# A fourth layer rebuilt in five stage lanes, with elementwise work moved off GpSimd

## The chip, the cores and the metric

The kernel runs on one NeuronCore of a Trainium2 chip. It is one launch: the residual goes in with channels first and comes out in the same form. The metric is the device time of that launch in microseconds, the median of several runs. The engines are called PE (TensorE matmul), PEld (its weight loads), DVE (VectorE), ACT (ScalarE), POOL (GpSimd) and SP (SyncE), as in the profile. All data are fp32.

## The reference

Four layers, each a macaron: half a feed-forward, a mixing block, half a feed-forward, with the residual `x` (4 batches of 1024 tokens, 128 channels) running through. Layers 0 to 2 are a mixture of experts with attention over heads, a gated feed-forward with attention over tokens, and a mixture of experts with decayed linear attention. The change is in layer 3:

```python
x = x + 0.5 * _L3_ffn_ref(_layernorm(x), ...)
x = x + _L3_attn_ref(_layernorm(x), ...)
x = x + 0.5 * _L3_ffn_ref(_layernorm(x), ...)

# _L3_ffn_ref: x_prev is x one token earlier
xr = mu_r * x + (1.0 - mu_r) * x_prev
xk = mu_k * x + (1.0 - mu_k) * x_prev
out = sigmoid(xr @ W_r.T) * (square(relu(xk @ W_k.T)) @ W_v.T)

# _L3_attn_ref: 16 heads of 8 channels
xx = xs - x                                   # xs is x one token earlier
m = tanh((x + xx * time_maa_x) @ time_maa_w1)       # five groups of 32
mw, mk, mv, mr, mg = einsum("btfe,fec->fbtc", m, time_maa_w2)
xw = x + xx * (time_maa_w + mw)               # xk, xv, xr, xg likewise
r, k, v = xr @ W_r, xk @ W_k, xv @ W_v
g = silu(xg @ W_g)
w = time_decay + tanh(xw @ time_decay_w1) @ time_decay_w2
# per token, S is 8x8 for each head, wd = exp(-exp(w)):
#   y = r . (S + u * k v);   S = S * wd + k v
yn = groupnorm(y) * ln_gamma + ln_beta
out = yn * g @ W_o
```

## The kernel before, in words

The residual lies in four SBUF tiles `X[b]` of 128 channels by 1024 tokens. Layer 3 works on halves of 512 tokens (`HALF`); I call one batch and one half a unit, so there are eight units, and half 1 of a batch follows half 0.

`normed` (L919) is a layer norm in this form: a product with the centering matrix, `Square` and a copy on ACT, four products of 128 tokens with a column of means (`n_sq`), `Sqrt` on ACT and a reciprocal on DVE, four products that spread the result over channels (`n_r`), and a DVE product that gives `xn`. Column 0 of `xn` is the last token of the half before (or zero), set by POOL, so that `xn[:, 0:512]` is "one token earlier".

`l3_ffn` (L959) does both halves of a batch: a norm, four products that mix the present and the past token in the weights, three ACT functions, one more product, a DVE product, and the addition to the residual on POOL (L984).

`l3_time` (L999) does a half in this order. `xx` on POOL (L1012), `xxx` on DVE, the low-rank products, and four products of 32 rows, `w2`, into four PSUM banks of the pool `wave`. `mixed` (L1027) forms each of the five inputs on DVE and then adds `x` on POOL (L1030). The projections give `wdec`, `k`, `vals`, `r`, `g`. Then the recurrence: the 8 x 8 state of the 16 heads is laid out as 8 columns `j` of 128 partitions each. For each of two waves, four products of 32 rows (`vrows`) spread a column of `vals` into four banks; for each of the four, DVE multiplies it with `k` (`kv`, L1066), a scan along the tokens gives the state `st` (L1072), POOL copies a column in (L1071) or out (L1076), and POOL multiplies `st` with `r` into `z` (L1078). Four products of 32 columns (`sums`) then add the `z` of a wave into quarters of one accumulator `acc`. The finish is a group norm on `y`, a product with `g` on POOL (L1101), two products with `W_o`, and the addition to the residual on DVE.

The order of the work is set in two steps. Each function is a generator that yields costs; `lanes` (L1111) always runs on the lane whose summed cost is lowest, and so fixes the order in which the program is written down. A planner then puts every engine's instructions into one fixed queue, earlier written ones first where it expects them to be ready; it lets layer 3's first instructions in between those of layer 2's last experts. On the chip each engine works its queue in order. In layer 3 there are two lanes (L1239 to L1246): batches 0 and 2 with their tiles on the left of SBUF, batches 1 and 3 on the right, each with two PSUM banks, and four banks (`wave`) shared. The mixture of experts of layer 2 has its tiles on the left and the four PSUM banks `main`; layer 2's attention and layer 1's feed-forward had their tiles on the right and the four banks `side`.

The last three parts of layer 2 are `experts` for batches 2 and 3 (39 blocks, each with a 578 KB weight load, L455, an indirect gather, L457, and an indirect scatter, L442) and `combine` (L476). Batches 0 and 1 have their final residual before these experts begin.

Of the kernel before, what the change touches and what calls it, by code (L numbers as in the profile page):

```python
# [12 lines left out]
AF = mybir.ActivationFunctionType  # L13
ALU = mybir.AluOpType
AX = mybir.AxisListType

P = 128
# [4 lines left out]
HALF = 512  # L22
# [183 lines left out]
class Macaron:  # L206
# [712 lines left out]
    def normed(self, ps, wp, b, h, before):  # L919
# [5 lines left out]
        sq, xc = self.t(wp, [P, HALF], "n_sq", bufs=1), self.t(wp, [P, HALF], "n_xc", bufs=1)  # L925
# [5 lines left out]
        std, r = self.t(wp, [P, 4], "n_std"), self.t(wp, [P, 4], "n_r")  # L931
# [5 lines left out]
        xn = self.t(wp, [P, HALF + 1], "xn")  # L937
        if before is None:
            nc.gpsimd.memset(xn[:, 0:1], 0.0)
        else:  # L940
            nc.gpsimd.tensor_copy(xn[:, 0:1], before[:, HALF:])
# [17 lines left out]
    def l3_ffn(self, ps, wp, m, b):  # L959
        nc = self.nc  # L960
        bank = lambda: self.t(ps, [P, HALF], "bank")
        xn = None
        for h in range(2):
            X = self.X[b][:, h * HALF : (h + 1) * HALF]
            xn = self.normed(ps, wp, b, h, xn)
            yield 3
            x, xp = xn[:, 1:], xn[:, 0:HALF]

            def mixed(k):
                o = bank()  # L970
                self.mm(o, m["now" + k], x, stop=False)
                self.mm(o, m["past" + k], xp, start=False)
                return o

            r, k, y = (self.t(wp, [P, HALF], tag, bufs=1) for tag in ("r", "k", "y"))
            k2 = self.t(wp, [P, HALF], "kv")
            nc.scalar.activation(k, mixed("k"), AF.Relu)
            nc.scalar.activation(k2, k, AF.Square)
            nc.scalar.activation(r, mixed("r"), AF.Sigmoid)
            yield 4  # L980
            o = bank()
            self.mm(o, m["wv"], k2)
            nc.vector.tensor_tensor(y, r, o, ALU.mult)
            nc.gpsimd.tensor_tensor(X, X, y, ALU.add)  # L984
            yield 2
# [13 lines left out]
    def l3_time(self, ps, wave, wp, m, c3, b):  # L999
        nc = self.nc  # L1000
        v, act, pool = nc.vector, nc.scalar.activation, nc.gpsimd
        bank = lambda shape=(P, HALF): self.t(ps, list(shape), "bank")
        four = lambda: [self.t(wave, [P, HALF], "wave") for _ in range(4)]
        one = lambda tag, rows=P, bufs=1: self.t(wp, [rows, HALF], tag, bufs=bufs)
        xn = carry = None
        for h in range(2):
            X = self.X[b][:, h * HALF : (h + 1) * HALF]
            xn = self.normed(ps, wp, b, h, xn)
            yield 3
            x, xp = xn[:, 1:], xn[:, 0:HALF]  # L1010
            xx, xxx = one("xx"), one("xxx")
            pool.tensor_tensor(xx, xp, x, ALU.subtract)  # L1012
            v.scalar_tensor_tensor(xxx, xx, m["maa"][:, 0:1], x, ALU.mult, ALU.add)
            lo, hi = one("lo"), one("hi", 32)
            lp = bank()
            self.mm(lp, m["w1"][:, 0:P], xxx)
            act(lo, lp, AF.Tanh)
            hp = bank((32, HALF))
            self.mm(hp, m["w1"][:, P : P + 32], xxx)
            act(hi, hp, AF.Tanh)  # L1020
            yield 4
            mp = four()
            for f in range(4):
                rows = slice(32 * f, 32 * f + 32)
                self.mm(mp[f], m["w2"][rows, :], lo[rows, :])

            def mixed(f, mp):  # L1027
                t = one("mix", bufs=3)
                v.scalar_tensor_tensor(t, mp, m["maa"][:, f + 1 : f + 2], xx, ALU.add, ALU.mult)
                pool.tensor_tensor(t, t, x, ALU.add)  # L1030
                return t
# [253 lines left out]
```

## Time and profile before

| | |
|---|---|
| median of 3 runs | 3297.95 us (3294.87 to 3299.5) |
| profiled execution | 3388.92 us |
| its span | 3387.1 us |
| granted TensorE clock over the span | 0.888 |
| PE, PEld, DVE | 2861.4, 1672.3, 1793.1 us busy |
| ACT, POOL | 1614.4, 973.6 us busy |

The profiled execution is about 2.8% longer than the runs without a profile. A row of groups gives the engine, the operation, what it writes and reads, the shape, the count, the busy time, the mean time of one, and the idle time of the engine ahead of them with what ended it. `x128` of a PE group counts two passes for each fp32 product. The profile tells two PE groups apart only by their tiles, since most products are written in one helper line (L227). Where busy times of several PE records overlap, the busy time is that of their union.

### The profile page before, as it was taken

The numbers are of one execution on the slowest core, as the hardware profiler recorded it, in microseconds if no ns is written. First come the engines' busy times: TensorE is split into PE (matmuls) and PEld (weight loads), VectorE is DVE, ScalarE is ACT, GpSimd is POOL, SyncE is SP. The second block draws the span as 40 slices with busy tenths as digits, with TensorE's granted clock in tenths as the row PEclk, the third lists the DMA queues.
The fourth block names the chain that finished last, engine by engine and source line by source line (L and its number), as shares of the span: only waits on it lengthen the run. The fifth ranks groups of instructions, "written<-read, shape, count | busy, mean of one in ns | idle before, by whom it ended". The sixth has DMA issues, their size and how long they took to land.

```text
span 3387.1 us, 48419 instructions
## 1 busy us (share of the span) xinstructions
PE 2861.4 (84%) x18126; PEld 1672.3 (49%) x18126; DVE 1793.1 (53%) x3048; ACT 1614.4 (48%) x3546; POOL 973.6 (29%) x972
## 2 busy tenths in 40 slices
PE   6777758778779999999999998987968877688887
PEld 6655547556533333333333335676757856223323
DVE  3387776853136776776776742434454422354353
ACT  4555525567404665665665663454423444322432
POOL 2465506433330000000000000353404444254353
PEclk7888959889879999999999998998978979687888
DMA  5565516544400000000000000475624656000000
GB/s 169 166 186 172 174 45 188 168 123 134 149 13 2 6 6 4 6 6 16 6 6 3 1 1 18 135 218 170 185 71 144 193 166 188 13 0 7 7 0 13
DMA packets 122890, 277.64 MB, mean 82 GB/s; under 512 B 18016, under 2 KB 67296, under 8 KB 122528
## 3 DMA queue, kind: packets, MB, share of 16 engines
q1 hardware_dynamic: 101792, 231.77, 23.1%
q0 software_dynamic: 20864, 42.77, 4.1%
q8 instruction: 144, 2.36, 0.3%
q14 instruction: 90, 0.74, 0.1%
HBM read 238.43 MB, written 31.85 MB: 80 GB/s over the span
## 4 chain that ended last, share of the span: by engine, by line
PE 68%; DVE 13%; POOL 5%; issue 5%; ACT 5%; DMA 4%; another core or an unknown queue 0%; SPq 0%; POOLq 0%; DVEq 0%; ACTq 0%
PE bank L227 37%; PE two L227 16%; PE o L227 8%; PE s L227 4%; DMA c_y<-res 2%; DVE nm L717 2%; POOL z L1078 1%; DMA res<-e_y,g_target 1%; DVE prod L542 1%; ACT e_h L468 1%; DVE sc L527 1%; POOL res L442 1%; DVE prod L525 1%; PE bank L461 1%; PE wave L227 1%
## 5 line engine op out<-in xcount | busy, mean ns | idle before, releaser
L717 DVE TENSOR_REDUCE nm<-two 128x2 f32<-128x1024 f32 x512 | 626.8, 1224 | 289.2 <-PE s L227 269.8
L740 ACT ACTIVATE e<-s 128x512 f32<-128x512 f32 x1024 | 555.8, 595 | 403.5 <-PE s L227 400.5
L468 ACT ACTIVATE e_h<-bank,e_w 128x128 f32<-128x128 f32 x1304 | 453.3, 367 | 544.2 <-PE bank L227 445.6
L227 PE MATMUL bank<-e_x,e_w 128*128 128x128 f32 x2608 | 573.0, 318 | 152.4 <-ACT e_h L468 61.5
L227 PE MATMUL s<-qm,kz 32*128 32x512 f32 x2048 | 633.5, 642 | 0.8 <-ACT e L740 0.8
L227 PE MATMUL two<-kz,qz 32*128 32x512 f32 x2048 | 592.1, 663 | 19.5 <-DVE nm L717 2.5
L457 POOL DMA_INDIRECT e_xg<-rows,g_source x326 | 328.5, 1008 | 942.1 <-DVE g_target L412 347.5
L227 PEld LDWEIGHTS bank<-e_x,e_w 128*128 128x128 f32 x2608 | 413.8, 203 | 290.4 <-ACT e_h L468 124.3
L442 POOL DMA_INDIRECT res<-e_y,g_target x326 | 376.1, 1154 | 319.5 <-DVE e_y L441 179.9
L227 PE MATMUL bank<-e_w,e_h 128*128 128x128 f32 x2608 | 450.7, 289 | 15.7 <-ACT e_h L468 12.9
L227 PEld LDWEIGHTS bank<-e_w,e_h 128*128 128x128 f32 x2608 | 378.4, 202 | 29.5 <-ACT e_h L468 22.3
L227 PE MATMUL o<-e,va 128*32 128x256 f32 x4096 | 328.3, 392 | 0.1
L441 DVE TENSOR_TENSOR e_y<-bank,e_w 128x128 f32<-128x128 f32 x326 | 94.4, 290 | 438.3 <-PE bank L227 379.5
L227 PEld LDWEIGHTS two<-kz,qz 32*128 32x128 f32 x2048 | 159.3, 188 | 237.5 <-issue 161.0
L227 PEld LDWEIGHTS o<-e,va 128*32 128x32 f32 x4096 | 81.0, 108 | 389.6 <-issue 370.3
L227 PEld LDWEIGHTS s<-qm,kz 32*128 32x128 f32 x2048 | 206.5, 183 | 11.4 <-issue 7.7
L705 POOL COPY va<-vd 128x256 f32<-128x256 f32 x16 | 6.7, 432 | 624.4 <-PE o L227 538.1
L463 DVE COPY e_x<-bank 128x128 f32<-128x128 f32 x326 | 92.8, 285 | 93.6 <-PE bank L461 73.2
L493 PE MATMUL bank<-c,c_y 128*128 128x128 f32 x128 | 39.5, 453 | 111.8 <-DVE c_y L490 111.8
L227 PE MATMUL bank<-g_cols,g_lanes 128*128 128x39 f32 (+1 forms) x512 | 83.3, 321 | 25.5 <-DVE g_cols L392 24.8
L1078 POOL TENSOR_TENSOR z<-st,r 128x512 f32<-128x512 f32 x64 | 96.0, 1503 | 22.7 <-DVE st L1072 22.4
L461 PE MATMUL bank<-c,e_xg 128*128 128x128 f32 x326 | 94.5, 290 | 7.6 <-DMA e_xg<-rows,g_source 7.6
(302 smaller groups left out, 3778.1 us busy)
## 6 DMA issues: line engine op xcount, KB each, us to landing
e_w<-in_l0m_dram SPq DMA_DIRECT2D x170, 578.0 KB
e_w<-in_l2m_dram SPq DMA_DIRECT2D x156, 578.0 KB
c_y<-res SPq DMA_DIRECT2D x32, 512.0 KB
rows<-g_xt SPq DMA_DIRECT2D x16, 512.0 KB
e_xg<-rows,g_source POOLq DMA_INDIRECT x326
res<-e_y,g_target POOLq DMA_INDIRECT x326
x<-in_x_dram SPq DMA_DIRECT2D x4, 512.0 KB
qz<-qd SPq DMA_DIRECT2D x64, 32.0 KB
```

Source lines behind the costliest of these rows:

```text
L227: self.nc.tensor.matmul(out, lhsT, rhs, start=start, stop=stop)
L441: nc.vector.tensor_tensor(y, o, w[:, MOE_W - D :], ALU.add)
L442: ins = nc.gpsimd.indirect_dma_start(out=res[:, :], out_offset=at(target[:, k : k + 1]), in_=y, in_offset=None)
L457: nc.gpsimd.indirect_dma_start(out=xg, out_offset=None, in_=rows[:, :], in_offset=at(source[:, k : k + 1]))
L461: nc.tensor.transpose(tp, xg, self.c0["ident"])
L463: nc.vector.tensor_copy(x, tp)
L468: nc.scalar.activation(h[:, fc, :], up[:, fc, :], func, bias=w[:, 2 * FC * P + fc : 2 * FC * P + fc + 1])
L493: nc.tensor.transpose(tp[:, j, :], y[1][:, i, :], self.c0["ident"])
L525: v.tensor_tensor(pr, q.unsqueeze(2).to_broadcast(sh), k.unsqueeze(1).to_broadcast(sh), ALU.mult)
L717: v.tensor_reduce(nm[:, it, h, 2 * pair : 2 * pair + 2], s, AX.X, ALU.max, negate=True)
L740: nc.scalar.activation(es[g], s, AF.Exp, scale=scale)
L1078: pool.tensor_tensor(z, st[:, 0:HALF], r, ALU.mult)
```

## The change

`l3_time` is cut into three functions, and layer 3 gets five lanes in place of two: one that runs the recurrences of all units, two for the ends of even and odd batches (`l3_finish` and the second feed-forward) and two for their fronts (the first feed-forward and `l3_prepare`). A lane's part is one unit, not one batch. A recurrence waits for its `prepare`, a finish for its recurrence.

Pools: the fronts' tiles lie on the right of SBUF and the recurrence's and the ends' on the left; PSUM has 2 banks for the broadcasts, 1 for `acc`, 2 shared by the ends, 3 shared by the fronts. `g` and `y` have two buffers, the other results of `l3_prepare` one for each of the two fronts.

Moved from POOL: `xx`, the residual addition of the feed-forward, the product with `g`, every second `z` and the memsets go to DVE; the column copies go to ACT. The addition of `x` in `mixed` is left out, and the weight is applied twice in one accumulation, once to `x` and once to the rest. The `w2` products come in pairs in place of fours, as do the broadcasts. A helper, `together`, ties a list of products to one another in PE's queue (and optionally behind another product); the sums of a wave come in fours, behind the next pair of broadcasts.

```diff
-    def normed(self, ps, wp, b, h, before):
+    def normed(self, ps, tmp, wp, b, h, before):
...
-        xn = self.t(wp, [P, HALF + 1], "xn")
+        xn = self.t(wp, [P, HALF + 1], "xn", bufs=3)
         if before is None:
-            nc.gpsimd.memset(xn[:, 0:1], 0.0)
+            nc.vector.memset(xn[:, 0:1], 0.0)
         else:
-            nc.gpsimd.tensor_copy(xn[:, 0:1], before[:, HALF:])
+            nc.scalar.copy(xn[:, 0:1], before[:, HALF:])
...
-            nc.vector.tensor_tensor(y, r, o, ALU.mult)
-            nc.gpsimd.tensor_tensor(X, X, y, ALU.add)
+        nc.vector.tensor_tensor(r, r, o, ALU.mult)
+        nc.vector.tensor_tensor(X, X, r, ALU.add)
...
+    def together(self, matmuls, after=None):
+
+        order = mybir.DependencyInfo(mybir.DependencyClass.NoSync, mybir.DependencyReason.DATA)
+        for out, lhsT, rhs, start, stop in reversed(matmuls):
+            i = self.nc.tensor.matmul(out, lhsT, rhs, start=start, stop=stop).ins
+            if after is not None:
+                self.tc.add_manual_dep(i, after.name, order, reason="side by side")
+            after = i
+        return after
...
+    def l3_prepare(self, ps, tmp, wp, m, c3, b, h, seen, out):
...
+        v.tensor_tensor(xx, xp, x, ALU.subtract)
...
+            if fs == (4,):
+                self.mm(mp[0], m["w2l"], hi)
+            else:
+                self.together([(mp[i], m["w2"][rows[i], :], lo[rows[i], :], True, True) for i in range(2)])
...
+        def project(w, share=None, rows=P, alone=None):
+            o = bank((rows, HALF))
+            if share is None:
+                self.mm(o, w, alone)
+            else:
+                self.mm(o, w, x, stop=False)
+                self.mm(o, w, share, start=False)
+            return o
...
+    def l3_recur(self, wave, ps, wp, c3, b, h, carries, given):
...
+        for w in range(2):
+            zs = []
+            for pair in range(2):
+                js = [4 * w + 2 * pair + i for i in range(2)]
+                vb = [self.t(wave, [P, HALF], "wave") for _ in js]
+                rows = [slice(32 * (j % 4), 32 * (j % 4) + 32) for j in js]
+                last = self.together([(vb[i], c3["vrows"][rows[i], w, :], vals[rows[i], :], True, True) for i in range(2)])
+                for sums in held:
+                    self.together(sums, last)
+                held = []
+                kv = []
+                for i in range(2):
+                    kv.append(self.t(wp, [P, HALF], "kv", bufs=3))
+                    v.tensor_tensor(kv[i], k, vb[i], ALU.mult)
+                for i, j in enumerate(js):
                     st = self.t(wp, [P, HALF + 1], "st", bufs=3)
-                    if last is None:
-                        pool.memset(st[:, 0:1], 0.0)
+                    if h == 0:
+                        v.memset(st[:, 0:1], 0.0)
                     else:
-                        pool.tensor_copy(st[:, 0:1], last[:, j : j + 1])
+                        nc.scalar.copy(st[:, 0:1], carry[:, j : j + 1])
                     v.tensor_tensor_scan(
...
                     if h == 0:
-                        pool.tensor_copy(carry[:, j : j + 1], st[:, HALF:])
-                    z = one("z", bufs=6)
-                    pool.tensor_tensor(z, st[:, 0:HALF], r, ALU.mult)
+                        nc.scalar.copy(carry[:, j : j + 1], st[:, HALF:])
+
+                    z = self.t(wp, [P, HALF], "z", bufs=6)
+                    (pool if i else v).tensor_tensor(z, st[:, 0:HALF], r, ALU.mult)
                     zs.append(z)
...
+            held.append([(acc[32 * q : 32 * q + 32, :], c3["sums"][:, w, :], zs[q], w == 0, w == 1) for q in range(4)])
+        for sums in held:
+            self.together(sums)
+        v.tensor_tensor(y, y, acc, ALU.add)
...
+    def l3_finish(self, ps, wp, m, c3, b, h, given):
...
-            pool.tensor_tensor(yc, yc, g, ALU.mult)
+        v.tensor_tensor(yc, yc, g, ALU.mult)
...
+    def layer3(self, f, t, c3):
...
+            wave, accs, tail, prep = (
+                enter(self.psum(name, n)) for name, n in (("l3wave", 2), ("l3acc", 1), ("l3tail", 2), ("l3prep", 3))
+            )
+
+            tmp, *front = (enter(sb(name, side="right")) for name in ("l3tmp", "l3even", "l3odd"))
+            rec, *end = (enter(sb(name)) for name in ("l3rec", "l3ends0", "l3ends1"))
...
+            units = [(b + i, h) for b in range(0, B, 2) for h in range(2) for i in range(2)]
+            fronts, recs, ends = ([], []), [], ([], [])
+            for b, h in units:
...
+            self.lanes(recs, *ends, *fronts)
```

## The prediction

> **What bounds the kernel now.** I read the page's forty slices first, then the table of stretches over the last 650 us, then the groups of the last layer, and last the timeline inside one recurrence. Times below are us from the span's start. The slices say where the kernel is weak:
>
> ```profile
> span 3387.1 us, 48419 instructions
> ...
> PE   6777758778779999999999998987968877688887
> ...
> PEclk7888959889879999999999998998978979687888
> ```
>
> A slice is 84.7 us, so the last six, from 2880 on, are the last layer. PE is at 6 to 8 tenths at a granted clock of 6 to 8 tenths there: it is neither full nor fast. I cut that part into stretches at the turns of the recurrence (the span in which `st` and `z` are made); columns are the length, then busy us and instructions of PE, PEld, DVE, ACT, POOL, then PEclk, DMA share, GB/s:
>
> ```profile
> 2735.00:2868.00 133.00, 114.64 (x738) 95.86 (x737) 25.59 (x87) 68.48 (x179) 72.58 (x77) 0.93 0.62 191
> ...
> 2888.00:2952.00 64.00, 49.27 (x116) 21.13 (x116) 12.34 (x21) 22.69 (x33) 13.69 (x16) 0.69 0.00 0
> 2952.00:3001.00 49.00, 35.59 (x89) 8.39 (x87) 35.93 (x39) 5.05 (x9) 35.25 (x50) 0.72 0.00 1
> ...
> 3088.00:3198.00 110.00, 100.08 (x358) 52.88 (x356) 28.54 (x49) 54.76 (x87) 25.66 (x32) 0.92 0.03 10
> ...
> 3284.00:3329.00 45.00, 31.29 (x76) 7.47 (x74) 34.95 (x37) 7.88 (x12) 31.69 (x27) 0.77 0.00 1
> ...
> 2888.00:3372.00 484.00, 394.52 (x1153) 157.40 (x1153) 217.13 (x278) 155.69 (x240) 210.46 (x241) 0.81 0.01 4
> ```
>
> The reader is to see three things. First, the recurrence (two of its four stretches are shown, 189 us in all four) in which DVE and POOL each work 70 to 78% and PE is granted about 0.73. Second, 64 us (2888 to 2952) before the first of them in which nobody is above 77% and PE gets 0.69. Third, 3088 to 3198, where two batches are in plain products and PE is at 91% with clock 0.92: that is what this layer can do when it has work from several places. Over 2888 to 3372 PE is 394.5 us busy at 0.81, 320 us of full clock in 484 us, 66%.
>
> Why the recurrence is slow is in the groups since 2800 (busy us, mean ns, then idle time before) and in the timeline (start, length, in us):
>
> ```profile
> L1078 POOL TENSOR_TENSOR z<-st,r 128x512 f32<-128x512 f32 x64 | 96.0, 1503 | 22.7 <-DVE st L1072 22.4
> ...
> L1072 DVE TENSOR_TENSOR_SCAN st<-wdec,carry,kv 128x512 f32<-128x512 f32 x32 | 45.9, 1463 | 0.1
> ```
> ```profile
> 2957.58 1.26 POOL L1078 TENSOR_TENSOR z<-st,r 128x512 f32<-128x512 f32 x1
> ...
> 2959.39 4.00 DVE L1072 TENSOR_TENSOR_SCAN st<-wdec,kv 128x512 f32<-128x512 f32 x2
> ...
> 2960.44 1.85 POOL L1030 TENSOR_TENSOR mix<-mix,xn 128x512 f32<-128x512 f32 x1
> ```
>
> A free scan takes 1.2 us, a free `z` 1.26. Here two scans take 4.00 with two Pool products beside them: scan and Pool product take turns, so a head costs about 1.2 + 1.27 us of two engines, and in order.
>
> **What the skill says.** "SBUF — State Buffer", section "SBUF: two separate sides": the second port pair is an exclusive lock between a GpSimd instruction and a DVE one with two SBUF inputs; the loser blocks for the whole instruction. The lines above agree. "TensorE: Matmul & The Clock Gate", Part 3, says that 32-row or 32-column products in different strips run at once if issued together; the trace agrees where they are together (eight `wave` records, four products, in 1.14 us at 2952.72) and shows the loss where they are not (one `z` product alone, 1.04 us at 3075.62). Part 1 of that page has the clock halved after some us of idleness; 0.69 against 0.92 above agrees in kind. "ScalarE: Activation LUTs", "What ACT_TABLE_LOAD costs": about 1283 ns[...], and the trace has 1283 ns.
>
> **The change, part by part.** A unit is one batch half, eight in all. One 128x512 product costs 0.86 us at full clock (starts at 3102.58 and 3103.44 of two products in a row); the eight small `n_sq` passes and the eight `n_r` passes about 0.95 each.
>
> *PE.* After, one unit has: three norms, each 0.86 + 0.95 + 0.95 = 2.76, so 8.3; two feed-forwards of five products, 8.6; `l3_prepare` with 2 (w1), 2 pairs (w2), 1 (w2l), 2 (dw1 and its share of x), 1 (dw2), 8 (four projections, each twice) and 1 (bonus), 17 x 0.86 = 14.6; the recurrence with four pairs of broadcasts and two fours of sums, 6 x 0.86 = 5.2; the finish, 3 x 0.86 and two times eight small passes, 4.5. Sum 41.2, times eight 330 us of full clock. Before, the same count has 5 products less (4.3) and one four instead of two pairs (0.6), but broadcasts and sums were issued as they came: 63.8 + 41.6 us busy in the four recurrence stretches, 13.2 a unit at about 0.73, so 9.6 instead of 5.2. That is 40.7. So projecting twice is paid for by `together`: PE's work stays, net +0.5 a unit. A lone product in a pair's place would cost 0.86; if no pair or four came together at all it would be 16 x 0.86 = 13.8, +69 us for the kernel.
>
> *POOL and DVE.* POOL loses 40 additions of 1.09, 32 of 64 `z`, 16 `x`, 8 `yc`, 8 `xx` and the column copies; it keeps 32 `z`, 32 x 1.27 = 41 us. DVE gets 32 `z`, 16 `x`, 8 `yc`, 8 `xx`, each a two-input SBUF product: 0.69 us (`qs<-q,grow`, the same form, takes 0.69 at 2500.98). Per unit DVE has: norms 3 x 0.9; feed-forwards 4 x 0.69; prepare 0.69 + 7 x 0.75 + 0.69 = 6.6; recurrence 8 kv x 0.65, 8 scans x 1.23, 4 z x 0.69, y 0.69, zeros 0.4 = 18.9; finish 0.55 + 3 x 0.69. Sum 33.6, eight units 269 us (217 before). Waits for a Pool `z`: after the pair's second scan DVE goes on to `kv`, which reads PSUM and ran beside a Pool product at 2957.55, so between 0 and 32 x 1.27 = 41 us; I take 20. The one-column memsets on DVE I have not seen; between 0.05 and 0.17 us (a 128x128 memset takes 0.17).
>
> *ACT.* It gets 64 column copies for `st` and `carry` and 12 for `xn`. Nearest row: `n_std`, 128x4, 0.26; between 0.15 and 0.3, so 11 to 23 us; I take 17. Table loads: about 43 since 2800, 55 us; with five lanes interleaved at most ten a unit, 80 x 1.28 = 103. ACT is then at most 156 + 17 + 48 = 221 of some 360 us: not the bound. But each column copy stands in ACT's queue behind a scan (`carry`) or a free `st`, and behind it stand the evictions of all other lanes.
>
> *The start.* Before, only the odd lane ran under the last experts (its norms at 2739, 2778, 2817) and stopped at `wave`, whose banks the experts held; the even lane, on the left of SBUF where the experts' tiles lie, began at 2885. That is 17 us of PE. After, both front lanes lie on the right, with three PSUM banks of their own, and end in `given`. Batches 0 and 1 are final at 2735, 133 us before the experts end. A front of a unit (norm, ffn, norm, prepare) is 2 x 2.76 + 4.3 + 14.6 = 24.4 us of PE, two are 49. PE has room: 35 blocks of 16 products at 0.11 and a transpose are about 70 us, with 17 of now 87 of 133. So the fronts of 00 and 10 go there. They delay the experts, since PE runs in order: between 0 and 25 us; I take 10.
>
> *The sum.* Combines end at 2888 + 10. PE has 330 - 49 = 281 us left, at clock 0.92 and 0.91 busy (the stretch 3088 to 3198) 281 / 0.84 = 336. DVE beside it has 269 - 20 + 20 = 269, 80% of that, so it fits but is the next bound. Tail: from the last `z` at 3329 to the end are 59 us, with 39 us of PE in it (38.4 x 0.87 + 7.5 x 0.71), worth 46 at that density; 13 lost. The new end is thinner, one unit instead of two, so 22. 2898 + 336 + 22 = 3256, 131 less than 3387.1. The profiled execution took 3388.9 (span and 1.8 around it), the median of the runs shown is 3297.95, 0.973 of it. Scaled, 127 less: **3170 us**.
>
> **Rivals.** (1) *Fronts are not hidden* (order or banks keep them off): 313 us of PE left, 373, so 2888 + 373 + 22 = 3283, 104 less, median 3197; I count it with the forecast. (2) *Better:* half 1 of batches 0 and 1 also gets part of its front under the experts and the tail overlaps: 3200, 187 less, 3116. For it: 46 us of PE room. Against: fronts keep one buffer of `k`, `r`, `vals`, `wdec`, so they wait for `recur`. (3) *PE is not packed better:* five lanes still meet in queues whose order is planned beforehand, and PE stays at 0.64 of full clock (309 of 484 by my count); 281 / 0.64 = 439, 2898 + 439 + 12 = 3349, 38 less, 3261. For it: DVE needs 80%, PE 84%, two nearly full engines in order. Against: 3088 to 3198. (4) *Slower:* ACT's queue ties the lanes together. A column copy waits for a scan; behind it wait evictions that PE's banks need (three for two fronts, two for two ends), so the lanes run in turn. A unit then costs 24 (189 / 8) + 32 (64 / 2) + 21 (43 / 2, the stretch from 3329 to 3372) = 77 us; 2888 + 616 - 64 + 16 = 3456, 69 more, 3365. It decides from (3387 - 16 - 2888) / 8 = 60 us a unit on. Against: that price counts no overlap at all, and the old kernel made 60 with two lanes and Pool in the chain.
>
> **Numbers.** Forecast with (1) 0.57, (2) 0.13, (3) 0.20, (4) 0.08, no change 0.02. Cases (1) to (3) are all faster by over 0.2%, which is about what a measurement of this kernel tells from none. The range, 3095 to 3265, leaves out half of (2) and the upper part of (3) with (4).
>
> **What would show it.** In the changed kernel: scans near 1.2 us and Pool `z` 32 times; fronts' `mix` and `wdec` before 2890 and the first scan there; sums in fours of about 1 us; PE over 85% at a clock over 0.85 from 2900 to 3200; DVE about 270 us in the layer. The forecast is wrong if the first scan comes after 2930, if ACT's wait for scans is among the longest, or if expert blocks stretch by over 25 us.

## The result, and the profile after

| | us |
|---|---|
| kernel before, median of 4 runs | 3298.72 (3294.87 to 3305.24) |
| changed kernel, median of 4 runs | 3263.59 (3262.23 to 3265.91) |
| ratio, 95% interval | 0.9891 (0.9871 to 0.991) |
| forecast | 3170 (3095 to 3265) |

The change gains 35 us where 128 were forecast. The profiled execution of the changed kernel took 3264.24 us (span 3262.4) and agrees with its median. That of before, 3388.9, did not agree with its own, and the first thing to settle is what in it was typical. The kernel before was profiled once more (`b0`, span 3295.8). These rows give, for the old profile, the new one of the same kernel, and the changed kernel, the four reads `c_y` of the last combine: min/median/max duration in ns, then the first and last start in us.

Before, first profile:
```profile
L484 SPq DMA_DIRECT2D c_y<-res x4: 360/418/583, 2870.2 to 2879.2; - x4
```
Before, second profile:
```profile
L484 SPq DMA_DIRECT2D c_y<-res x4: 359/416/584, 2779.4 to 2788.5; - x4
```
The changed kernel:
```profile
L484 SPq DMA_DIRECT2D c_y<-res x4: 360/419/584, 2765.0 to 2774.0; - x4
```

From the first of these reads to the end of the span is a stretch that holds the last combine and all of the last layer that isn't under the experts. It is 516.9 us in the first profile of before, 516.4 in the second, 497.4 in the changed kernel. So the 91 us by which the two profiles of one kernel differ lie ahead of it, in stages that the diff doesn't touch. Chips differ in their times: on those used below the kernel before takes 3294 to 3299 us (two of them) or 3371 to 3385 us (two others). Which chip the first profile came from isn't recorded; its total is of the second kind, and its last layer is sound. The stretch is therefore a second measure for what follows, beside the times. It comes from one profile of each run, and that it doesn't change with the chip is known from these two profiles alone. It was 495.7 in a second profile of the changed kernel (`e12`).

The changed kernel gains 19 us in the stretch, and 14.4 us ahead of it. The second part is no gain of the last layer's work. Here are the windows of before (second profile) and after for the last experts, the last combine, and the layer to near its end: length, busy us and instructions of PE, PEld, DVE, ACT and POOL, then PEclk, DMA share and GB/s.

Before, second profile:
```profile
2667.00:2779.00 112.00, 101.19 (x699) 86.28 (x697) 23.73 (x82) 63.21 (x167) 72.18 (x79) 0.98 0.73 226
2779.00:2800.00 21.00, 7.44 (x28) 5.51 (x29) 7.13 (x21) 7.38 (x20) 0.00 (x0) 0.50 0.36 100
2800.00:3285.00 485.00, 395.25 (x1151) 157.36 (x1151) 217.02 (x277) 155.44 (x239) 210.42 (x241) 0.81 0.01 4
```
The changed kernel:
```profile
2663.00:2765.00 102.00, 95.00 (x654) 79.42 (x652) 18.54 (x75) 55.43 (x154) 68.01 (x70) 1.00 0.79 249
2765.00:2785.00 20.00, 6.09 (x18) 3.44 (x19) 7.61 (x28) 5.08 (x17) 0.00 (x0) 0.50 0.39 105
2785.00:3250.00 465.00, 429.15 (x1275) 179.93 (x1274) 249.54 (x381) 191.67 (x339) 46.21 (x32) 0.87 0.01 4
```

The last experts are 10 us shorter while *less* of the last layer runs beside them: 654 PE records against 699. `e1` below has 744 and the stage is longer, so the two go together. And the layer itself is a new picture. GpSimd fell from 210 to 46 us, scans no longer wait for it (median 1.22 or 1.27 us), and PE went from 82% busy at clock 0.81 to 92% at 0.87. PE is now by far the fullest engine. It has about 373 us of full-clock work in that window (429.15 x 0.87, busy time by the mean clock), where the forecast left it 281. Where this work is, the groups of before (second profile, window 2785 to 3262) and after (window 2785 to 3262) show (busy us, mean ns, idle before).

Before, second profile:
```profile
L227 PE MATMUL bank<-z,attn_c 128*32 128x512 f32 x128 | 67.2, 871 | 33.6 <-POOL z L1078 33.6
...
L227 PE MATMUL wave<-vals,attn_c 32*128 32x512 f32 x128 | 43.9, 780 | 3.7 <-DVE kv L1066 3.5
...
L227 PE MATMUL wave<-lo,attn_w 32*128 32x512 f32 x64 | 12.4, 649 | 0.0
```
The changed kernel:
```profile
L1004 PE MATMUL wave<-vals,attn_c 32*128 32x512 f32 x128 | 67.1, 697 | 6.1 <-DVE kv L1095 6.1
L227 PE MATMUL bank<-xn,attn_w 128*128 128x512 f32 x64 | 39.7, 706 | 0.8 <-DVE mix L1041 0.8
...
L1004 PE MATMUL bank<-t,attn_w 32*128 32x512 f32 x64 | 25.4, 684 | 0.0
...
L1004 PE MATMUL acc<-z,attn_c 128*32 128x512 f32 x128 | 23.2, 742 | 2.9 <-POOL z L1109 2.9
```

The fours of sums did come together: 16 of them in 23.2 us, against 67.2 in before. Most pairs did not. 64 broadcasts take 67.1 us, no less than 64 single ones at 1.05, and 32 `w2` products take 25.4. Before, in fours, the same products took 43.9 and 12.4 us. So what the sums gained, the broadcasts and `w2` lost: the three groups are 123.5 us at a mean clock of 0.81 before and 115.7 at 0.87 after, about 100 us of full-clock work both times. The timeline of PE shows why (start and length in us, `x2` is one fp32 product):

```profile
2858.88 1.06 PE L1004 MATMUL acc<-z,attn_c 128*32 128x512 f32 x8
2859.87 1.12 PE L1004 MATMUL wave<-vals,attn_c 32*128 32x512 f32 x2
2860.93 1.05 PE L227 MATMUL bank<-c,n_sq 128*128 128x1 f32 x8
2861.91 1.12 PE L1004 MATMUL wave<-vals,attn_c 32*128 32x512 f32 x2
```

Four sums share 1.06 us. Two broadcasts have a full-array norm between them, and each costs 1.1 us of its own (2.1 us where the clock is at half). `together` adds dependencies that say which product is issued *after* which, not that nothing may come between, and the planner puts other work between them. In the compiled order about 14 of 32 pairs of broadcasts are neighbours and 10 of 16 `w2` pairs; in the trace 12 pairs of broadcasts overlap.

The last difference is at the layer's start:

```profile
2676.96 1.02 PE L227 MATMUL bank<-xn,past_r 128*128 128x512 f32 x2
...
2782.09 0.48 PE L493 MATMUL bank<-c,c_y 128*128 128x128 f32 x1 [0.38 <-DVE c_y L490]
2783.96 2.08 PE L227 MATMUL bank<-xn,now_k 128*128 128x512 f32 x2 [1.39 <-DVE xn L941]
```

Both front lanes make the products of their first norm, the even one also four products of its feed-forward by 2678, and stop: 9 us of PE work (two norms of 2.76 and four products of 0.86), where the forecast had 49. The next product of a front, the odd lane's first, comes at 2784, right behind the last combine. The first scan follows at 2840.7. So the fronts were hardly hidden. The memory map of the compiled kernel names the cause: the odd front pool (143008 to 182016 bytes in each partition) reaches 7744 bytes into the experts' pool (up to 150752), and its `xn` lies where the last combine's `c_y` lies. That lane holds one of three shared PSUM banks while it waits for the last combine, and the even lane's next bank comes behind it in the ring.

### The profile page after: what moved, and what is told of

It is laid out like the page before. It is cut to its first block, busy times and chain, and to the rows that moved or that the text cites. A ratio compares the mean times of both kernels' runs of the same rounds, so it can differ in the third digit from the quotient of the medians.

```text
span 3262.4 us, 48511 instructions
## 1 busy us (share of the span) xinstructions
PE 2850.0 (87%) x18206; PEld 1660.8 (51%) x18206; DVE 1820.2 (56%) x3156; ACT 1640.6 (50%) x3632; POOL 805.4 (25%) x748
## 5 line engine op out<-in xcount | busy, mean ns | idle before, releaser
L227 PE MATMUL bank<-e_x,e_w 128*128 128x128 f32 x2608 | 560.9, 312 | 110.4 <-DVE e_x L463 43.4
L457 POOL DMA_INDIRECT e_xg<-rows,g_source x326 | 336.8, 1033 | 876.8 <-DVE g_target L412 346.6
L227 PEld LDWEIGHTS bank<-e_x,e_w 128*128 128x128 f32 x2608 | 401.8, 197 | 238.1 <-ACT e_h L468 94.7
L442 POOL DMA_INDIRECT res<-e_y,g_target x326 | 369.5, 1134 | 282.9 <-DVE e_y L441 147.8
L227 PE MATMUL bank<-e_w,e_h 128*128 128x128 f32 x2608 | 435.4, 284 | 4.0 <-ACT e_h L468 2.3
L227 PEld LDWEIGHTS bank<-e_w,e_h 128*128 128x128 f32 x2608 | 366.3, 197 | 15.2 <-ACT e_h L468 11.6
L1109 POOL TENSOR_TENSOR z<-st,r 128x512 f32<-128x512 f32 x32 | 46.2, 1444 | 403.3 <-DVE st L1102 240.3
L227 PE MATMUL bank<-g_cols,g_lanes 128*128 128x39 f32 (+1 forms) x512 | 75.7, 303 | 24.4 <-DVE g_cols L392 24.4
```

The source lines that it names most:

```text
L227: self.nc.tensor.matmul(out, lhsT, rhs, start=start, stop=stop)
L442: ins = nc.gpsimd.indirect_dma_start(out=res[:, :], out_offset=at(target[:, k : k + 1]), in_=y, in_offset=None)
L457: nc.gpsimd.indirect_dma_start(out=xg, out_offset=None, in_=rows[:, :], in_offset=at(source[:, k : k + 1]))
L1109: (pool if i else v).tensor_tensor(z, st[:, 0:HALF], r, ALU.mult)
```

## The experiments

Theory: the gain that was missed is (a) the fronts, which stand still for that overlap, and (b) PE work, from pairs that don't come together and from projecting twice. Rivals: the chain over VectorE and ScalarE sets the layer, so PE work is worth little; adjacent pairs bring nothing; GpSimd still holds up the rest. All times are medians beside the kernel before on the same chip; "stretch" is the one defined above. Runs were made in groups, each with its own runs of before, and differences of up to some 10 us between groups are no finding: the changed kernel itself stood 35.1 us below before at first and 25.8 in `e12`.

| run | us | before beside it | difference | ratio (95%) | stretch |
|---|---|---|---|---|---|
| changed kernel | 3263.59 | 3298.72 | -35.1 | 0.9891 (0.9871 to 0.991) | 497.4 |
| e12, the same again | 3268.66 | 3294.43 | -25.8 | 0.9917 (0.9892 to 0.9941) | 495.7 |
| e1 fronts | 3215.73 | 3299.1 | -83.4 | 0.976 (0.9728 to 0.9791) | 429.2 |
| e2 pairs | 3276.54 | 3299.1 | -22.6 | 0.9932 (0.9914 to 0.995) | 509.1 |
| e3 both | 3236.88 | 3299.1 | -62.2 | 0.9809 (0.9787 to 0.9832) | 443.6 |
| e4 no second product | 3226.59 | 3295.34 | -68.8 | 0.98 (0.9777 to 0.9824) | 458.8 |
| e5 x added on VectorE | 3264.96 | 3295.34 | -30.4 | 0.9906 (0.9884 to 0.9928) | 494.8 |
| e6 pairs by priority | 3268.27 | 3295.34 | -27.1 | 0.9921 (0.99 to 0.9942) | 502.2 |
| e7 fronts, x on GpSimd | 3200.21 | 3295.34 | -95.1 | 0.971 (0.9687 to 0.9733) | 415.2 |
| e8 half the broadcasts, tight | 3335.96 | 3385.43 | -49.5 | 0.9854 (0.9825 to 0.9882) | 475.3 |
| e9 half the broadcasts, loose | 3323.09 | 3385.43 | -62.3 | 0.9807 (0.9776 to 0.9838) | 455.4 |
| e10 no order | 3338.16 | 3385.43 | -47.3 | 0.9857 (0.983 to 0.9883) | 478.8 |
| e16 no order again | 3327.78 | 3370.78 | -43.0 | 0.9875 (0.9847 to 0.9902) | 480.8 |
| e11 as e7, all z on VectorE | 3283.22 | 3385.43 | -102.2 | 0.969 (0.9666 to 0.9715) | 409.5 |
| e13 fronts, no order | 3213.96 | 3294.43 | -80.5 | 0.9748 (0.9722 to 0.9775) | 426.7 |
| e14 as e7, no order | 3216.04 | 3294.43 | -78.4 | 0.9767 (0.9741 to 0.9793) | 428.9 |
| e15 as e14, all z on VectorE | 3224.42 | 3294.43 | -70.0 | 0.9788 (0.9763 to 0.9812) | 434.7 |
| e17 fronts, x on VectorE | 3281.37 | 3370.78 | -89.4 | 0.9738 (0.9713 to 0.9764) | 424.4 |

**b0, the kernel before once more.**

> The kernel before, unchanged, profiled a second time. If the profiled execution of before was untypical, and its excess lay in layers 0 to 2, this execution has a span near 3297, its last group of expert weight loads starts near 2660 (as in the changed kernel) rather than at 2741, and the stretch from the first last-combine read to the end is again about 517 us. If the change itself shortened the earlier layers, the span is near 3387 again and the last experts start near 2741.

Span 3295.8, the last experts' loads begin at 2667.0, the stretch is 516.4: the first profile was the untypical one, and only ahead of the last layer.

**e1, the fronts freed.**

```diff
-                ts.append(one("mix", bufs=3))
+                ts.append(one("mix", bufs=2))
...
-        dt = one("t4", 64)
+        dt = one("t1", 64)
```

> The changed kernel with two SBUF economies in the preparation (the decay's inner tile shares t1, mix gets two buffers instead of three), so that the odd front pool no longer lies over the last combine's c_y. Theory (the fronts stood still because of this overlap): several dozen PE products of the first two units run under the last experts, the first scan starts within 25 us of the end of the last combine instead of 57, and the time falls by 15 to 35 us, to 3229 to 3249. Rival (TensorE is the bound in the experts too, so work moved there only lengthens them): the experts' stage grows by what the fronts take, and the time stays within 8 us of 3264. Second rival (fewer mix buffers stall the preparation): slower than 3272.

In the compiled kernel both front pools now lie above the experts' pool (the lower begins at 151200). The time falls by 48 us, more than expected. Windows of the last experts, the last combine and the layer, then PE's timeline and the first scan on VectorE:

```profile
2663.00:2781.00 118.00, 114.45 (x744) 90.37 (x743) 32.91 (x95) 67.16 (x180) 68.38 (x70) 1.00 0.69 216
2781.00:2801.00 20.00, 18.55 (x58) 7.20 (x57) 11.61 (x34) 13.43 (x28) 0.00 (x0) 1.00 0.39 105
2801.00:3200.00 399.00, 367.93 (x1149) 156.29 (x1149) 233.90 (x355) 167.03 (x303) 45.97 (x32) 0.89 0.01 4
```
```profile
2692.06 1.02 PE L227 MATMUL bank<-xn,past_r 128*128 128x512 f32 x2
...
2723.11 1.02 PE L227 MATMUL bank<-t,attn_w 128*128 128x512 f32 x2
...
2741.58 1.12 PE L1004 MATMUL bank<-t,attn_w 32*128 32x512 f32 x2
...
2748.24 1.07 PE L227 MATMUL bank<-xn,attn_w 128*64 128x512 f32 x2
```
```profile
2801.40 2.33 DVE L1102 TENSOR_TENSOR_SCAN st<-wdec,kv 128x512 f32<-128x512 f32 x2
```

Under the experts both lanes now make their feed-forward products, and the even one goes on through `w1` and `w2`. The experts take 117 us instead of 102 (744 PE records instead of 654): 16 us longer, where the forecast took 10 and at most 25. The combine, in which the changed kernel's PE was 30% busy at clock 0.50, is 93% busy at clock 1.00. The first scan starts at 2801 instead of 2841, and the stretch is 68 us shorter. This is the largest cause, and it is shown: two tiles' room was worth more than the whole change had gained. Not all of the 48 us need be hiding: in this kernel's other order 17 pairs of broadcasts overlap in place of 12, and they take 61.5 us in place of 67.1.

**e2, e3 and e6, the pairs forced together.**

In `e2` and `e3` the pair's two banks are one tile, with one buffer of it:

```diff
-                vb = [self.t(wave, [P, HALF], "wave") for _ in js]
+                both = self.t(wave, [P, 2, HALF], "wave")
+                vb = [both[:, i, :] for i in range(2)]
```

In all three, `together` puts a pair at high priority for the planner (`e3` has the edit of `e1` too):

```diff
+        with ExitStack() as ctx:
+            if len(matmuls) == 2:
+                ctx.enter_context(self.tc.high_priority())
             for out, lhsT, rhs, start, stop in reversed(matmuls):
```

> The changed kernel with the two broadcasts of a pair written to the two banks of one two-bank tile and given a higher priority in the planner (w2 pairs and fours of sums get the priority for pairs alone), so that 30 of the 32 broadcast pairs are neighbours on TensorE's queue instead of about 14. Theory (broken pairs cost the gain): the broadcasts' busy time falls from 67 to about 33 us, w2 from 25 to about 20, and since TensorE is over 90% busy in layer 3 the time falls by 20 to 40 us, to 3224 to 3244. Rival (the chain over VectorE and ScalarE sets layer 3): TensorE gets idle instead, and the time stays within 8 us of 3264. Second rival (both banks free at once is later than one at a time): the scans wait longer and it is slower than 3272.

> Both edits together. Theory: the two gains are of different stretches and add up: 35 to 70 us below the changed kernel, 3194 to 3229. If TensorE isn't the bound or one edit's gain hides the other's, less than the larger of the two alone plus 8 us.

> The changed kernel with the planner's priority for pairs alone and the two wave banks as separate tiles, as in the changed kernel: 25 broadcast pairs are neighbours instead of about 14 of 32. If the two-bank tile (which comes free only when both products are read) was what made the pairs' experiment 13 us slower, this one is faster than the changed kernel by 5 to 25 us, 3239 to 3259. If it was the priority (broadcasts ahead of the preparation and the ends of other units on TensorE's queue), it is slower too, 3268 to 3285. If adjacent pairs are worth nothing since TensorE waits anyway, within 5 us of 3264.

The pairs came together and it did not help. Groups of `e2` in its layer, window 2792 to 3270:

```profile
L1007 PE MATMUL wave<-vals,attn_c 32*128 32x512 f32 x128 | 40.9, 703 | 12.5 <-DVE kv L1099 7.7 <-DVE st L1103 4.6
L1007 PE MATMUL bank<-t,attn_w 32*128 32x512 f32 x64 | 22.2, 700 | 0.0
L1007 PE MATMUL acc<-z,attn_c 128*32 128x512 f32 x128 | 21.4, 713 | 9.1 <-POOL z L1113 9.0
```
```profile
2792.00:3270.00 478.00, 412.81 (x1276) 175.69 (x1275) 249.62 (x381) 186.17 (x334) 47.38 (x32) 0.86 0.01 4
```

The broadcasts fell by 26 us of busy time, as hoped. PE's idle time in the window rose from 36 to 65 us. The third column says where in part: ahead of a pair PE now waits for `kv` and `st` (12.5 us, where it was 6.1), and ahead of a four for GpSimd's `z` (9.1, where it was 2.9); the rest is spread over other products. PE takes its queue in order: in the trace of the changed kernel the layer's 664 products start in the compiled order, but for a few neighbours that overlap. So, as we read it, a pair at its head that isn't ready holds everything behind it, where a single broadcast went out as soon as one bank was read. The stretch is 12 us longer (509.1), and with the fronts freed 14 (443.6 against 429.2; 21 us in the time). With the banks left separate (`e6`) it is 502.2, and its time is 5 us above the changed kernel's first, at the edge of what was to mean "worth nothing". In the time `e2` and `e6` can't be told from the changed kernel. The theory that unpaired products are lost time that these orders can win back has fallen. Broadcasts and `w2` in fours, as before had them, were not tried in the new lanes.

**e8 and e9, what the missing pairs weigh.**

```diff
-                vb = [self.t(wave, [P, HALF], "wave") for _ in js]
+                vb = [self.t(wave, [P, HALF], "wave")] * 2
...
-                last = self.together([(vb[i], c3["vrows"][rows[i], w, :], vals[rows[i], :], True, True) for i in range(2)])
+                last = self.together([(vb[i], c3["vrows"][rows[i], w, :], vals[rows[i], :], True, True) for i in range(1)])
```

In `e8` the pool `l3wave` also has one bank instead of two.

> The changed kernel with the second broadcast of each pair left out (both products with k read the first one's bank, so this part of the computation is left out) and one wave bank in place of two. TensorE does what it would do if all pairs came together at no cost in order, and the next broadcast waits, as with a two-bank pair, until both products have read. If broken pairs are what TensorE lost, their busy time falls from 67 to about 33 us, and the time by 25 to 40 us, to 3224 to 3239, as removing 40 whole products did (37 us). If a bank that comes free late is what makes it wait, as in the first pairs' experiment, less than 12 us: 3252 or more.

> As the one before, with the two wave banks kept, so that the next broadcast can be made while the last one is read. Broken pairs the cost: 25 to 40 us faster than the changed kernel here too, 3224 to 3239, and within 8 us of the tight one. Wave banks the cost: this one is more than 12 us faster than the tight one.

Both ran on a chip where before takes 3385 us, so their absolute times stand against that. The stretch is 22 us shorter than the changed kernel's with one wave bank and 42 with two; the gain over before grows by 14 to 24 us and by 27 to 37, by which run of the changed kernel one takes. So the work of the broadcasts does count. Between the two, which ran on one chip, lie 20 us of stretch and 13 in the medians, but `e9` was profiled in one of its quicker executions (3307.95 of 3306.6 to 3327.4), and the intervals of the ratios overlap: that a bank free in time is worth this is likely, not shown. PSUM's eight banks are all given out (2, 1, 2 and 3), and no experiment gave the broadcasts more.

**e10, e16 and e13, no order at all.**

```diff
-        for out, lhsT, rhs, start, stop in reversed(matmuls):
-            i = self.nc.tensor.matmul(out, lhsT, rhs, start=start, stop=stop).ins
-            if after is not None:
-                self.tc.add_manual_dep(i, after.name, order, reason="side by side")
-            after = i
-        return after
+        for out, lhsT, rhs, start, stop in matmuls:
+            self.mm(out, lhsT, rhs, start=start, stop=stop)
+        return None
```

> The changed kernel without the order of pairs and fours (the same products, issued by the planner as it likes): 3 of the 16 fours of sums stay whole. The sums' busy time should grow from 23 towards the 67 us of the kernel before. If TensorE's throughput sets layer 3, 25 to 45 us slower, 3289 to 3309, about the time of the kernel before; if the order itself costs as much as the pairs bring, within 8 us of 3264.

> The changed kernel, unchanged, as a control beside the next three: 33 to 38 us below the kernel before on the same chip (ratio 0.987 to 0.991), TensorE's granted clock in layer 3 again 0.86 to 0.88, and 490 to 500 us from the first read of the last combine to the end.

> The changed kernel without the order of pairs and fours, as before. If the order is a loss in itself, again 40 to 55 us below the kernel before (ratio 0.983 to 0.988). If the 12 us belonged to the other chip, 22 to 38 us below (0.9885 to 0.9935), as the changed kernel.

> The fronts' edit without the order of pairs and fours. If the order costs what it seemed to (about 12 us), 55 to 65 us below the changed kernel beside it, as the fronts alone were 48 below; TensorE's clock in layer 3 near 0.92. If the 12 us were the chip's, 43 to 53 below. If the sums' fours are worth what the forecast took (27 us at least), 20 to 30 below only.

The control `e12` is 25.8 us below before, less than the 33 expected, with clock and stretch as expected. Without the order the kernel is not slower, where 25 to 45 us were expected if PE's throughput sets the layer. Groups of `e10` (window 2885 to 3344) and its layer:

```profile
L227 PE MATMUL wave<-vals,attn_c 32*128 32x512 f32 x128 | 53.2, 662 | 0.8 <-DVE kv L1092 0.8
L227 PE MATMUL acc<-z,attn_c 128*32 128x512 f32 x128 | 42.4, 667 | 1.3 <-DVE z L1106 0.7 <-POOL z L1106 0.5
```
```profile
2885.00:3332.00 447.00, 417.32 (x1274) 172.24 (x1273) 249.62 (x381) 190.88 (x338) 43.16 (x32) 0.92 0.01 4
```

The sums do cost 19 us more, and the broadcasts 14 less: left alone, the planner issues more of them side by side (19 pairs overlap, in place of 12). The two groups together have 88 us of full-clock work (95.6 x 0.92) against 79 with the order (90.3 x 0.87). That is all the order is worth, 1.2 us in a unit, and PE waits a little less without it (30 us against 36) and runs at a higher clock (0.92 against 0.87). The stretch is 478.8 and 480.8 in two runs, against 497.4 and 495.7. In the time the gain over the changed kernel, 8 to 22 us, is from different chips, and the intervals overlap. The stretches compared are from different chips too: both runs without the order were on the slower kind, where the changed kernel was not measured. So a gain from dropping the order is not shown; the loss of 25 to 45 us that was expected is excluded. With the fronts freed the order makes no difference (`e13` against `e1`, 426.7 against 429.2).

**e4, e5, e7 and e17, projecting twice.**

```diff
-                self.mm(o, w, x, stop=False)
-                self.mm(o, w, share, start=False)
+                v.tensor_tensor(share, share, x, ALU.add)
+                self.mm(o, w, share)
```

That is `e5`. In `e4` the addition is left out, in `e7` and `e17` the fronts are freed as in `e1`, and in `e7` the addition is GpSimd's.

> The changed kernel with the second projection's product of x left out and nothing in its place: each of the five projections of a unit takes the mixed part alone, so x is missing from them and this part of the computation is left out. It prices TensorE: 40 products of 512 columns, 0.86 us each at the full clock, 34 us (39 us at the granted 0.87), are gone and no other engine does anything more. If TensorE's throughput sets layer 3, the time falls by 30 to 42 us, to 3222 to 3234. If the chain through VectorE and ScalarE sets it, as the pairs' experiment suggests in part (26 us less of broadcasts, and 13 us slower), it falls by less than 15, to 3249 or more, and TensorE shows gaps and a lower clock.

> The changed kernel with projecting twice undone and the addition of x made by VectorE: 40 products fewer (34 us at the full clock), 40 additions of about 0.69 us more on VectorE (28 us), each in the chain ahead of its projection. TensorE the bound: 3225 to 3242, close to the run without any addition. VectorE or the chain the bound: the additions cost what the products did, 3256 to 3290.

> The fronts' edit, with projecting twice undone and the addition of x made by GpSimd, as the kernel before did: against the fronts' run (3216) 40 products fewer on TensorE and 40 operations of about 1.3 us (52 us) on GpSimd, which is busy 46 us of 400 there. TensorE the bound and the fronts far enough ahead to hide GpSimd's latency: 15 to 30 us faster than 3216, 3186 to 3201. If GpSimd's work holds up VectorE by the shared port, as in the kernel before, or the longer chain of the preparation is late for its scans: 3216 or slower.

> The fronts' edit, one projection, x added by VectorE. TensorE still the bound: below the fronts alone (3216) by 10 to 25 us. The exchange of 40 products for 40 additions in the chain as even as in the changed kernel (3265 against 3264): 3208 to 3224.

Leaving the 40 products out takes 37 us off the time and 39 off the stretch, for 34 us of full-clock work (40 x 0.86). PE's work is paid for at about one to one here: the rival that the VectorE and ScalarE chain alone sets the layer has fallen in that form. But putting the additions on VectorE gives all of it back (`e5`). The layer of `e4` and of `e5`:

```profile
2785.00:3210.00 425.00, 385.07 (x1193) 166.78 (x1192) 247.75 (x381) 186.97 (x336) 45.14 (x32) 0.84 0.01 4
```
```profile
2793.00:3255.00 462.00, 408.95 (x1194) 172.35 (x1192) 269.37 (x421) 184.20 (x334) 46.38 (x32) 0.81 0.01 4
```

In `e5` VectorE has 22 us more to do and is still at 58%. PE has 331 us of full-clock work (408.95 x 0.81) against 323 in `e4`, 53 us of idle time against 40, and a lower clock. So it isn't VectorE's throughput either. Our reading is that each addition makes the chain from `mix` to its projection longer; the windows show that PE stands idle for longer, and that what it does takes longer at the lower clock. Projecting twice is an even exchange with additions on VectorE. With the fronts freed, GpSimd, which has become idle, can do the additions: `e7` is the fastest kernel measured beside before on a chip of 3295 us, 3200.21. Its stretch is 14 us shorter than `e1`'s and its gain over before 12 us larger, from two chips and with intervals that just overlap. VectorE in the same place (`e17`) lies between the two, and the intervals overlap.

**e11, e14 and e15, what adds up.**

> The fronts' edit with one projection and x added by GpSimd (3200), and now all of z on VectorE: 32 products of 0.67 us (21 us) more on VectorE, which is busy 235 of 384 us, and the sums no longer wait for GpSimd. If the sums' waits for GpSimd's z matter: 5 to 15 us faster, 3185 to 3195. If VectorE's work is in the chain of the scans: 5 to 15 us slower, 3205 to 3215.

> The fronts' edit, no order, one projection with x added by GpSimd. If the three costs add: 48 + 12 + 16 = 76 us below the changed kernel beside it, 70 to 82. If TensorE is no longer the bound by then (the same products of x are gone already): 60 to 68, no more than fronts and projection together.

> As the one before with all of z on VectorE. GpSimd's z holds up the sums or VectorE: 5 to 12 us below the one before. VectorE in the scans' chain: up to 10 us above it.

All `z` on VectorE (`(pool if i else v)` becomes `v`) gives a stretch of 409.5 after `e7`'s 415.2, 0.969 against 0.971: no difference that these runs can tell. Leaving out the order as well makes `e7` slower by 14 us in the stretch and 17 in the difference to before (`e14`), and `z` on VectorE doesn't mend it (`e15`). The gains don't add: without the order the sums stand alone again, and why this hurts only here was not tried.

## Why the prediction was wrong

- **The base.** The sum started from the profile's 3387.1 and was scaled by 0.973 to the median. The excess was not spread over the kernel: it lay ahead of the last layer. Taken off as it was, 91 us, the forecast end of 3256 is 3165, and the size of the gain stays about what it was, 131. So this step put a wrong label on the difference but isn't where the forecast failed.
- **"So the fronts of 00 and 10 go there".** This step failed, and it is the largest. The premise that both front lanes lie on the right with three PSUM banks of their own was true. Not asked was whether the right side reached below the top of the experts' pool. It did, by 7744 bytes, so the fronts stood still as in rival (1), and of the 17 us that before had hidden 8 were lost too. The forecast's own sign of this came: the first scan is at 2840.7, which is 2946 in the times of the first profile (105.2 us later at the last combine), past the 2930 it had named. Freed, the fronts gave 48 us, with 16 us of delay to the experts where the forecast took 10. Rival (1) priced it at 27 us, which was too small: the first scan also comes 40 us earlier, and PE is busy through the combine.
- **PE's work in a unit.** "Four pairs of broadcasts and two fours of sums, 5.2" measured 9.8 ((67.1 + 23.2) x 0.87 / 8), and the `w2` pairs 2.8 instead of 1.7. That is 45 us for eight units. Most of the 57 us by which PE's total came out too high is here (330 forecast; about 387: 373, 4 in the tail, and 9 for two norms and four products under the experts). `e4` shows that PE work is paid for at about one to one. The forecast had named the price of lone products, but took a dependency for adjacency, and it split the fours of broadcasts and of `w2`, which had run at 43.9 and 12.4 us, into pairs. That the orders tried don't bring this back is shown by `e2`, `e3` and `e6`; what the missing products weigh is 22 to 42 us of the stretch (`e8` and `e9`).
- **"Projecting twice is paid for by `together`".** This failed. `together` paid 1.2 us a unit (`e10`), not the 4.4 of the forecast. That projecting twice is even against additions on VectorE (`e5`) is another comparison, which the forecast didn't make.
- **GpSimd and VectorE.** Right. Scans take 1.22 and 1.27 us; GpSimd is at 46 us (41 forecast, its `z` at 1.44 in the mean); VectorE is at 250 in the window, with 269 forecast for the whole layer. A one-column memset takes 0.059 us.
- **ScalarE.** Its load was right: 192 us, column copies 0.19 each, 54 table loads in the layer (40 in before, at most 80 forecast). But its two longest waits are those of the column copies, `st` for a free buffer (35.7 us in all) and `carry` for scans (30.5), which the forecast had named as a sign of rival (4). No run took these copies off ScalarE, so what part rival (4) has stays open; little of PE's waiting ends at them (8.9 us of its weight loads wait for `carry`).
- **PE's density and the tail.** 0.91 x 0.92 forecast; 0.92 x 0.87 measured, and 0.92 x 0.89 with the fronts freed. Before it was 0.82 x 0.81. So the lanes did pack PE better, and rival (3), which put the time at 3261, next to what was measured, has no support: it kept PE at 0.64 of full clock and hid the fronts. That the time lies just within the forecast's range is luck in the same sense, since the slow end of the range stood for rival (3). From the last `z` to the end PE's work leaves 17 us unused (48 less 33.1 x 0.78 / 0.84), 22 forecast.

From 3170 to 3264 are 94 us. The fronts account for 48 by experiment, which leaves `e1` at 3216. The other 46 are of the size of the mis-sized term for pairs. That this term is their whole cause was only argued, since density and tail moved too: of it, what `e8` and `e9` took away by leaving work out is the part that was tried.

## What to carry to other kernels

Before you count work as hidden under an earlier stage, look at the memory map: a pool on the other side hides little if its tiles reach by a few kilobytes onto those that the earlier stage frees last, and one lane that waits so stops its neighbours through a shared ring of banks. A dependency that orders two products doesn't make them neighbours, and forcing neighbours on an engine that works in order exchanges busy time for waiting. Price a removed operation by leaving it out and by putting it elsewhere: in `e4` and `e5` the first said 37 us and the second nothing.

## What was not expected of the hardware

- The same kernel takes 3294 to 3299 us on two chips and 3371 and 3385 on two others. In the two profiles of before, one with a total of each kind, the last layer is the same (516.9 and 516.4 us). 37 us of the difference are there by the start of layer 1's scores (986.6 instead of 949.4; 993.8 in `e10`, on one of the slower chips). The scores take 1010 us in all three, and 54 us come after them and ahead of the last combine. So the difference lies in the layers that load experts' weights, or beside them.
- The clock that PE is granted ranged from 0.81 to 0.92 in the layer, at 86 to 94% busy, and it doesn't follow the busy share alone: 0.87 at 92% in the changed kernel, 0.84 at 91% with 34 us of work removed (`e4`), 0.92 at 93 to 94% in `e10`, `e13` and `e16`, 0.86 at 94% in `e15`. These are means: the trace's record of the clock holds only full and half. In the changed kernel's layer (2785 to 3250) 19 stretches at half begin, of 3.4 to 10.2 us each. 15 of them follow directly on 3.4 us in which PE was busy for 77% or less, the other four on 3.4 us with 92% or more. The Trainium skill, "TensorE: Matmul & The Clock Gate", Part 1, has the clock gate follow how busy PE was over windows of some 3.4 us, halving the clock after an idle one. The 0.50 in the changed kernel's combine agrees with that. In the layer no idle time of PE reached 3.4 us (the longest was 2.96), and the clock was halved all the same. So short pauses seem to cost clock as well as time; what halved it after the four full windows was not settled.
